# A top-p search on ScalarE: shorter arithmetic after each try, and two values made on VectorE

## The chip, the cores and the metric

The kernel runs on one core of a Trainium2 chip. The metric is the device time of one execution in microseconds (us), the median of several runs. Beside it stands one profiled execution, whose trace gives the start and length of every instruction.

Engines are named as the profile names them: PE (TensorE), PEld (its weight loads), DVE (VectorE), ACT (ScalarE), POOL (GpSimd), SP (SyncE). Each runs its own instructions in order and waits for others by semaphores.

## The reference

Two graph layers on N = 2708 nodes with D = 256 features, in float32. Cut to what matters:

```python
x = layernorm(x + relu(concat([x, adj @ x]) @ weight + bias))    # layer 0
R = adj + I;  R = R / R.sum(-1)
Xf = Xa = x
for n in range(2):                                               # layer 1
    q = Xa @ W1.T @ W2.T;  k = Xa @ W3.T
    probs = softmax(q @ k.T)                                     # N x N
    # nucleus (top-p): keep the largest probs of a row until their sum reaches 0.9
    A = probs * mask;  A = A / A.sum(-1)
    Xf = R @ Xf;  Xa = A @ Xa
    Z += Xf @ U1[n].T + Xa @ U2[n].T
h = layernorm(x + Z) * ln_g + ln_b
out = layernorm(x + h)
```

The part at issue is the mask of the second step (n = 1). It needs, for every row, the threshold at which the kept values reach 0.9 of the row's sum, without sorting 2708 values.

## The kernel before

Rows are worked on in 22 blocks of 128 rows (the last has 20). Block number t has a tile of 20 columns (`Block`, tile name `st` in the profile), one float per row and column: `z` (the row's sum of exponentials), `rz` (1/z), `nz` (-z), `l0`, `l1`, `l2` (three guesses, each z divided by the threshold guessed), `u0`, `u1` (l times the share of the row's sum that a try finds above its threshold), `n`, `kept`, `few`, `d`, `m` and others. All operations on them are one element wide. This tile has five buffers.

**The search of a block.** `begin_search` (VectorE, L893 to L898) makes `z`, `rz`, `nz` and the first guess `l0`. Two tries follow on ScalarE (`try_act`). A try k has two passes over the block's 2708 exponentials: L1027, Relu(e * l - z), and L1030, Sign of the same, each with a sum over the row (`relu`, `sign`). From these sums small operations make the next guess:

- L1033: n = 0.5 * sign + N/2
- L1035: u = relu * rz + n
- L1040: kept = l * (keep + 0.9 * slope) - down
- L1041: next l = -slope * u + kept
- L1043, in the second try alone: few = 0.9 * l1 - FEW

`keep`, `slope` and `down` are constants, one set for each try (`STEPS`). After that `last_level` (VectorE, L1064 to L1074) chooses the final level from `relu`, `rz`, `few` (L1064), `l1`, `u1` (L1066) and `l2`, and further values (L1068 on), and makes `d`. `below_level` (L1084) is a pass of VectorE over the block with `d`. Then VectorE takes candidates (L1091), sorts them (L1100, L1103), finds the threshold (L1119 to L1139), marks (L1144) and masks (L1149). L1149 writes the masked block that TensorE transposes (L562) and multiplies (L591).

**The loop and its order.** The order is written by hand. In period `per` the kernel has ScalarE try block per+1, VectorE finish the level of block per and the threshold of block per-1, TensorE multiply block per-2, and ScalarE form the exponentials of block per+2. A period has six slots g. In slot 0 ScalarE runs the first Relu pass, in slot 1 the first Sign pass and the small operations, in slots 2 and 3 the same of the second try. `begin_search` of block per+2 stands at the end of VectorE's slot 5, after `mask`; L882 (`shift`, the row maximum that the next exponentials L885 need) follows it in slot 0. Between its own work ScalarE copies TensorE's transposes out of PSUM (L564), one copy for each slot; TensorE can't go on without them.

**Beside it.** TensorE also works on the product R @ Xf in small units (L788). The rows for it are gathered by GpSimd (L745, DMA_INDIRECT, seven for a block of R). In the periods from 11 on GpSimd also does four operations of the last layer norm in a period (L1265, L1266), after which VectorE takes their statistics (L1240). SP issues the plain loads and stores.

**The first three blocks.** Block 0 makes its first try on VectorE (`try_dve`), its second try's sums partly on each, and `next_level` on ScalarE. `begin_search` of blocks 0, 1 and 2 runs ahead of the loop, around 706 to 716 us.

Of the kernel before, what the change touches and what calls it, by code (L numbers as in the profile page):

```python
# [11 lines left out]
AF = mybir.ActivationFunctionType  # L12
ALU = mybir.AluOpType
# [4 lines left out]
TOP_P = 0.9  # L18
# [15 lines left out]
STEPS = ((0.97048, 13.37709, 72.87486), (1.01755, 9.09506, 145.60103))  # L34
FEW = 17.8171
# [27 lines left out]
def gnn_two_layer_kernel(ctx: ExitStack, tc: tile.TileContext, N, xT_d, x_d, adj_d, w0_d, b0_d,  # L63
# [72 lines left out]
    with fast:  # L136
        fast_path(fast, tc, c, flags, fint, xT_d, x_d, w0_d, b0_d, w1_d, w2_d, w3_d, u1_d, u2_d, g_d, b_d)
# [22 lines left out]
def fast_path(ctx, tc, c, flags, fint, xT_d, x_d, w0_d, b0_d, w1_d, w2_d, w3_d, u1_d, u2_d, g_d, b_d):  # L160
    nc = tc.nc
    N, D, DA, NB, DC, KH, CHS, rows = c.N, c.D, c.DA, c.NB, c.DC, c.KH, c.CHS, c.rows
# [33 lines left out]
    b0 = es[1][:, :D]  # L196
# [328 lines left out]
    def logits(s, t, i):  # L525


        p = rows(t)
        lg = ps_lg()
        cs = KPS[2 * i:2 * i + 2]  # L530
        skip = CH - (cs[0][1] - cs[0][0])
        for h, (a, b) in enumerate(cs):
            o = slice(DA * h, DA * h + DA)
            at = (skip, 0)[h]
            nc.tensor.matmul(lg[:p, h, at:at + b - a], lhsT=q[o, t * P:t * P + p], rhs=keys[s][o, i, :b - a],  # L535
                             start=True, stop=True)
        a, b = cs[0][0], cs[-1][1]
        return lg.rearrange("p h n -> p (h n)")[:p, skip:skip + b - a], a, b
# [88 lines left out]
    def exps1(t):  # L627

        p = rows(t)
        e = es[t % 4]  # L630
        nmax, srt = st1[t]
        z = small.tile([P, 2], FP, tag="z1", name="z1", bufs=3)
        st1[t] = (srt, z)
        h = 11 * P

        def part(i):
            if i == 0:
                nc.scalar.activation(srt[:p], srt[:p], AF.Exp, bias=nmax[:p], scale=1.0)
            a, b = ((0, h), (h, N))[i]
            nc.scalar.activation(e[:p, a:b], e[:p, a:b], AF.Exp, bias=nmax[:p], scale=1.0,  # L640
                                 accum_out=z[:p, i:i + 1])
        return part
# [206 lines left out]
    def e2(t):  # L849
        return ring[t % 5]  # L850
# [40 lines left out]
    def begin_search(b):  # L891

        nc.vector.tensor_reduce(b.z, b.all[:b.p, :NL], AX.X, ALU.add)  # L893
        yield
        nc.vector.reciprocal(b.rz, b.z)
        nc.vector.tensor_scalar(b.nz, b.z, -1.0, None, op0=ALU.mult)
        yield
        nc.vector.tensor_scalar(b.l0, b.roots, b.roots, b.rz, op0=ALU.mult, op1=ALU.mult)  # L898

    def run_all(steps):  # L900
        for _ in steps:
            pass
# [22 lines left out]
    part = exps1(0)  # L925
# [5 lines left out]
    part = exps1(1)  # L931
# [11 lines left out]
    for t in range(NB):  # L943
        acc = ps_acc(t)
        part = exps1(t + 2) if t + 2 < NB else None
        b = None
        if t >= NB - 3:
            b = blocks[t - (NB - 3)] = Block(t - (NB - 3))
# [44 lines left out]
    scale, turn_out, project = ends  # L993
# [28 lines left out]
    def try_act(b, k, part):  # L1022


        e = e2(b.t)[:b.p, :N]
        if part == 0:
            nc.scalar.activation(scr[:b.p, :N], e, AF.Relu, bias=b.nz, scale=b.l[k], accum_out=b.relu)  # L1027
            return
        if part == 1:
            nc.scalar.activation(scr[:b.p, :N], e, AF.Sign, bias=b.nz, scale=b.l[k], accum_out=b.sign)  # L1030
            return
        if part == 2:
            nc.scalar.activation(b.n, b.sign, AF.Identity, bias=halfn[:b.p], scale=0.5)  # L1033
            return
        nc.scalar.activation(b.u[k], b.relu, AF.Identity, bias=b.n, scale=b.rz)  # L1035
        next_level(b, k)

    def next_level(b, k):
        keep, slope, down = STEPS[k]
        nc.scalar.activation(b.kept, b.l[k], AF.Copy, scale=keep + TOP_P * slope, bias=-down)  # L1040
        nc.scalar.activation((b.l1, b.l2)[k], b.u[k], AF.Identity, bias=b.kept, scale=-slope)  # L1041
        if k:
            nc.scalar.activation(b.few, b.l1, AF.Copy, scale=TOP_P, bias=-FEW)  # L1043

    def level(b, l):

# [275 lines left out]

    b0, b1, b2 = (blocks[t] for t in range(3))
    run_all(begin_search(b0))
    try_dve(b0, 0)
    run_all(begin_search(b1))
    try_dve(b0, 1)
    run_all(begin_search(b2))
    try_act(b0, 1, 0)
    next_level(b0, 1)  # L1330
    lg = logits(1, 3, 0)
    r_units(CC + 1)
    r_outs()
# [2 lines left out]
    for per in range(NB + 2):  # L1336
# [13 lines left out]
        for g in range(NG):  # L1350
# [26 lines left out]
            if b_act:  # L1377
                for k, part in {0: ((0, 0),), 1: ((0, 1), (0, 2), (0, 3)), 2: ((1, 0),), 3: ((1, 1), (1, 2), (1, 3))}.get(g, ()):
                    try_act(b_act, k, part)
# [19 lines left out]
    for f in later[0] + later[1]:  # L1399
# [10 lines left out]
                                   op0=ALU.mult, op1=ALU.is_lt)  # L1410
# [394 lines left out]
```

## Time and profile before

| | us |
|---|---|
| median of 6 runs (1255.69 to 1258.49) | 1256.62 |
| the profiled execution | 1256.08 |
| its span, first to last instruction | 1254.3 |
| TensorE busy in it | 1189.8 (95%) |
| VectorE busy | 975.4 (78%) |
| ScalarE busy | 734.7 (59%) |
| GpSimd busy | 637.5 (51%) |

| group | count | mean ns of one |
|---|---|---|
| L1027, L1030 ScalarE, 128x2708 | 41, 40 | 2641, 2642 |
| L1033 / L1035 / L1040 / L1041 / L1043 ScalarE, 128x1 | 40 / 40 / 41 / 41 / 21 | 294 / 386 / 186 / 295 / 187 |
| L895 / L896 / L898 VectorE, 128x1 | 21 / 21 / 21 | 164 / 134 / 273 |
| L1084, L1149 VectorE, 128x2720 | 21, 21 | 3041, 3055 |
| L745 GpSimd gather of `v_d` rows | 154 | 1281 |

How to read it: the shares are averages over the whole execution. The search runs only from about 700 us on; before that the first layer and the first step fill the time. Busy times of PE come from a model of pipelined matmuls. A line of the timeline has the start and the length in us, the engine, the line of the kernel, the operation, the tile written and the tiles read; a bracket at its end tells how long the engine had been idle and who ended that. An instruction's length reaches beyond the moment at which the engine takes up the next one, so that lengths of neighbours can overlap.

### The profile page before, as it was taken

To read this page: it belongs to the slowest core of one execution; us is meant where nothing else is said; L and a number is where in the kernel's file an instruction comes from. 1 tells how busy PE (TensorE), PEld (TensorE's weight loads), DVE (VectorE), ACT (ScalarE), POOL (GpSimd) and SP (SyncE) were. 2 spreads that over 40 slices of the span, in tenths; PEclk is the share of its full clock that TensorE was granted. 3 is DMA by queue.
4 is the path that set the end of the run, shared out by engine and by line. 5 is a ranking of instruction groups with operands and counts; after the bars stand their busy time and mean duration, and the time that the engine had idled before them with its cause. 6 is when DMAs were issued, how large, how long until landed. Compare 5 with 4: busy or idle time off the path is not lost.

```text
span 1254.3 us, 18668 instructions
## 1 busy us (share of the span) xinstructions
PE 1189.8 (95%) x5772; PEld 905.4 (72%) x5772; DVE 975.4 (78%) x3254; ACT 734.7 (59%) x1299; POOL 637.5 (51%) x596
## 2 busy tenths in 40 slices
PE   8999999999899999999999989999999999999885
PEld 6888878863477777777777667777766777766763
DVE  2455555784999998988861488989999999988796
ACT  2010110125466566666665498989989899988721
POOL 1000000004555552677676588788807888888850
PEclk9999999999899999999999999999999999999987
DMA  8475445433322220132334555655615555554441
GB/s 201 153 208 172 148 148 174 135 112 120 101 66 81 74 76 13 46 105 88 95 87 120 153 185 180 189 166 179 177 36 188 179 155 174 178 157 151 147 115 31
DMA packets 104248, 164.92 MB, mean 131 GB/s; under 512 B 20162, under 2 KB 76870, under 8 KB 104138
## 3 DMA queue, kind: packets, MB, share of 16 engines
q1 hardware_dynamic: 77852, 107.57, 26.9%
q0 software_dynamic: 20544, 51.17, 15.0%
q10 hardware_dynamic: 5742, 4.89, 1.4%
q8 instruction: 48, 0.79, 0.3%
q14 instruction: 62, 0.51, 0.1%
HBM read 129.66 MB, written 33.90 MB: 130 GB/s over the span
## 4 chain that ended last, share of the span: by engine, by line
PE 47%; ACT 8%; DVE 2%; POOL 2%; issue 1%; DMA 1%; POOLq 0%; ACTq 0%
PE acc L591 22%; PE misc L788 9%; PE lg L535 6%; PE tr L562 6%; ACT e L1030 2%; ACT e L885 1%; ACT e L1027 1%; PE misc L727 1%; POOL yg L745 1%; DVE e L1149 1%; PE acc L699 1%; ACT u L1250 1%; ACT wT L564 1%; ACT e L889 1%; DMA yg<-v_d,ix 1%
## 5 line engine op out<-in xcount | busy, mean ns | idle before, releaser
L564 ACT COPY wT<-tr 128x512 f32<-128x512 f32 (+2 forms) x258 | 136.6, 537 | 193.5 <-PE tr L562 193.4
L745 POOL DMA_INDIRECT yg<-v_d,ix x154 | 197.3, 1281 | 75.8 <-DMA v_d<-base 30.4
L591 PE MATMUL acc<-ya,wT 128*128 128x256 f32 x924 | 226.9, 388 | 0.0
L591 PE MATMUL acc<-x,wT 128*128 128x256 f32 x882 | 218.7, 388 | 0.0
L745 POOL DMA_INDIRECT yg<-yf_d,ix x154 | 188.9, 1227 | 55.8 <-issue 22.1
L274 PE MATMUL acc<-y,adj_t 128*128 128x257 f32 x924 | 204.4, 379 | 0.0
L591 PEld LDWEIGHTS acc<-x,wT 128*128 128x128 f32 x882 | 160.0, 191 | 59.2 <-issue 25.5
L591 PEld LDWEIGHTS acc<-ya,wT 128*128 128x128 f32 x924 | 174.1, 193 | 38.9 <-issue 16.7
L274 PEld LDWEIGHTS acc<-y,adj_t 128*128 128x128 f32 x924 | 173.6, 189 | 26.8 <-issue 1.9
L384 POOL DMA_INDIRECT adj_t<-in_adj,ix x154 | 164.5, 1068 | 51.6 <-issue 44.1
L562 PE MATMUL tr<-ident,e 128*128 128x128 f32 (+1 forms) x946 | 146.7, 274 | 17.2 <-DVE e L1149 12.1
L788 PE MATMUL misc<-yg,adj_t 128*128 128x256 f32 (+1 forms) x602 | 157.0, 389 | 0.9 <-DMA yg<-v_d,ix 0.8
L562 PEld LDWEIGHTS tr<-ident,e 128*128 128x128 f32 (+1 forms) x946 | 118.8, 143 | 51.3 <-issue 17.0
L535 PE MATMUL lg<-k,q 64*128 64x512 f32 (+3 forms) x528 | 136.5, 594 | 18.7 <-ACT e L889 7.6
L351 POOL DMA_DIRECT2D part_d<-e x1 | 0.6, 573 | 272.6 <-DVE e L350 272.6
L788 PEld LDWEIGHTS misc<-yg,adj_t 128*128 128x128 f32 (+1 forms) x602 | 104.7, 188 | 38.4 <-issue 16.8
L1027 ACT ACTIVATE e<-e,st 128x2708 f32<-128x2708 f32 (+1 forms) x43 | 113.6, 2641 | 0.0
L1030 ACT ACTIVATE e<-e,st 128x2708 f32<-128x2708 f32 (+1 forms) x42 | 111.0, 2642 | 0.0
L462 ACT COPY x1T<-tr 128x256 f32<-128x256 f32 (+1 forms) x22 | 8.0, 365 | 174.6 <-PE tr L461 174.6
L597 DVE MAX8 cand<-e 128x8 f32<-128x170 f32 (+1 forms) x352 | 86.3, 318 | 14.6 <-ACT e L542 14.5
L1091 DVE MAX8 cand<-w 128x8 f32<-128x170 f32 (+1 forms) x352 | 94.1, 321 | 0.1
L535 PEld LDWEIGHTS lg<-k,q 64*128 64x128 f32 (+1 forms) x528 | 38.9, 181 | 50.5 <-issue 20.9
(254 smaller groups left out, 1794.5 us busy)
## 6 DMA issues: line engine op xcount, KB each, us to landing
adj_t<-in_adj SPq DMA_DIRECT2D x42, 704.0 KB
adj_t<-adjc_d SPq DMA_DIRECT2D x44, 448.0 KB
adjc_d<-adj_t SPq DMA_DIRECT2D x22, 256.0 KB
base<-za_d SPq DMA_DIRECT2D x40, 128.0 KB
adjc_d<-adj_t SPq DMA_DIRECT2D x22, 192.0 KB
xt<-in_x ACTq DMA_DIRECT2D x21, 128.0 KB
x_d<-x SPq DMA_DIRECT2D x21, 128.0 KB
x1b_d<-xb SPq DMA_DIRECT2D x21, 128.0 KB
```

Source lines behind the costliest of these rows:

```text
L274: nc.tensor.matmul(acc[:p, :n], lhsT=halves[k // KH][:, k % KH, :p], rhs=y[:, k, :n], start=k == 0, stop=stop and k == NB - 1)
L384: nc.gpsimd.indirect_dma_start(out=a[:CW, i, :], out_offset=None, in_=adj_rows, in_offset=bass.IndirectOffsetOnAxis(ap=ix[:CW, m, i:i + 1] ...
L535: nc.tensor.matmul(lg[:p, h, at:at + b - a], lhsT=q[o, t * P:t * P + p], rhs=keys[s][o, i, :b - a], start=True, stop=True)
L562: nc.tensor.transpose(tr[:, k % 4, :p], columns(e[:p], k), ident[:p, :p])
L564: nc.scalar.copy(wT[:, :len(ks), :p], tr[:, :len(ks), :p])
L591: nc.tensor.matmul(acc[:p, :D], lhsT=wT[:, k % 4, :p], rhs=part_y(y, k), start=k == 0, stop=k == NB - 1)
L597: nc.vector.max(dst[:p, i * 8:(i + 1) * 8], src[:p, i * step:i * step + w])
L745: nc.gpsimd.indirect_dma_start(out=yg[:CW, m % 3, i, :], out_offset=None, in_=rows_d, in_offset=bass.IndirectOffsetOnAxis(ap=ix[:CW, m, i: ...
L788: nc.tensor.matmul(acc[:p, :D], lhsT=a[:kw, k, :p], rhs=y[:kw, k, :] if k < CC else own[:p], start=k == 0, stop=k == CC)
L1027: nc.scalar.activation(scr[:b.p, :N], e, AF.Relu, bias=b.nz, scale=b.l[k], accum_out=b.relu)
L1030: nc.scalar.activation(scr[:b.p, :N], e, AF.Sign, bias=b.nz, scale=b.l[k], accum_out=b.sign)
L1091: nc.vector.max(b.cand[:p, 8 * i:8 * i + 8], low[:p, SEG2 * i:SEG2 * (i + 1)])
```

## The change

In the first try ScalarE no longer forms u0. VectorE makes two values ahead, in `begin_search`: m = -slope * rz, and d = l0 * (keep + 0.9 * slope) - down - slope * N/2, in columns that the block has already. ScalarE then makes n = -slope/2 * sign + d and l1 = m * relu + n, which is the former l1 with its terms in another order. The operations `kept` (of the second try's constants) and `few` need only l1 and now come right after it, at the end of the first try (`from_level`). The second try then ends in n, u1 and l2. For one block ScalarE has seven small operations instead of nine, and VectorE two more. For blocks 0, 1 and 2 the two operations of VectorE are added ahead of the loop as well; block 0 doesn't use them.

```diff
@@ begin_search
         yield
+        keep, slope, down = STEPS[0]
         nc.vector.tensor_scalar(b.l0, b.roots, b.roots, b.rz, op0=ALU.mult, op1=ALU.mult)
+        nc.vector.tensor_scalar(b.m, b.rz, -slope, None, op0=ALU.mult)
+        nc.vector.tensor_scalar(b.d, b.l0, keep + TOP_P * slope, -down - slope * N / 2, op0=ALU.mult, op1=ALU.add)
@@ try_act
+        if part == 2 and k == 0:
+            nc.scalar.activation(b.n, b.sign, AF.Identity, bias=b.d, scale=-STEPS[0][1] / 2)
+            return
         if part == 2:
             nc.scalar.activation(b.n, b.sign, AF.Identity, bias=halfn[:b.p], scale=0.5)
             return
-        nc.scalar.activation(b.u[k], b.relu, AF.Identity, bias=b.n, scale=b.rz)
-        next_level(b, k)
-
-    def next_level(b, k):
-        keep, slope, down = STEPS[k]
-        nc.scalar.activation(b.kept, b.l[k], AF.Copy, scale=keep + TOP_P * slope, bias=-down)
-        nc.scalar.activation((b.l1, b.l2)[k], b.u[k], AF.Identity, bias=b.kept, scale=-slope)
-        if k:
-            nc.scalar.activation(b.few, b.l1, AF.Copy, scale=TOP_P, bias=-FEW)
+        if k == 0:
+            nc.scalar.activation(b.l1, b.relu, AF.Identity, bias=b.n, scale=b.m)
+            from_level(b)
+            return
+        nc.scalar.activation(b.u1, b.relu, AF.Identity, bias=b.n, scale=b.rz)
+        nc.scalar.activation(b.l2, b.u1, AF.Identity, bias=b.kept, scale=-STEPS[1][1])
+
+    def from_level(b):
+        keep, slope, down = STEPS[1]
+        nc.scalar.activation(b.kept, b.l1, AF.Copy, scale=keep + TOP_P * slope, bias=-down)
+        nc.scalar.activation(b.few, b.l1, AF.Copy, scale=TOP_P, bias=-FEW)
@@ before the loop
     try_act(b0, 1, 0)
-    next_level(b0, 1)
+    from_level(b0)
+    nc.scalar.activation(b0.l2, b0.u1, AF.Identity, bias=b0.kept, scale=-STEPS[1][1])
```

## The prediction

> **What bounds the kernel now.** I read the table of stages first, then the waits of each engine, then the chain of waits in order of time, then the timeline of single instructions. The change lives in the loop over 22 row blocks that begins near 721 us. In the table of stages the columns are: stretch, its length, then busy time (and instructions) of PE, PEld, DVE, ACT, POOL, then granted clock, DMA share and GB/s.
>
> ```profile
> 721.70:764.20 42.50, 34.43 (x149) 24.94 (x148) 33.89 (x115) 38.09 (x57) 34.28 (x28) 0.96 0.59 181
> 764.20:943.50 179.30, 178.26 (x878) 137.19 (x877) 165.00 (x564) 161.50 (x262) 120.09 (x98) 1.00 0.52 155
> 943.50:964.10 20.60, 18.08 (x89) 12.86 (x88) 18.52 (x64) 19.90 (x34) 16.64 (x14) 1.00 0.53 171
> 964.10:1018.00 53.90, 53.90 (x271) 42.40 (x269) 51.38 (x179) 49.42 (x82) 43.22 (x39) 1.00 0.58 179
> 1018.00:1089.40 71.40, 69.52 (x339) 52.95 (x339) 69.66 (x235) 68.52 (x115) 59.75 (x51) 1.00 0.55 161
> 1089.40:1191.70 102.30, 92.32 (x440) 72.41 (x438) 88.80 (x311) 87.77 (x154) 85.19 (x72) 0.97 0.52 160
> ```
>
> The reader is to see five regimes. 721.7 to 764.2 and 943.5 to 964.1: ScalarE is busiest (38.1 of 42.5, 19.9 of 20.6) and TensorE has gaps; the chain of waits passes through ScalarE's small operations at 727, 735, 749, 946 and 954 us. 764.2 to 943.5 and 964.1 to 1018: TensorE has hardly a gap (178.3 of 179.3, 53.9 of 53.9). 1018 to 1089.4: VectorE is busy 69.7 of 71.4, more than any other. From 1089.4 no engine is full, so a loop through several must bind. The waits of VectorE in the second and the sixth row tell the difference (total, times, longest):
>
> ```profile
> DVE st L1064 <- ACT st L1043: 8.7, 8, 1.5
> DVE bst L1240 <- POOL u L1266: 12.0, 8, 2.2
> ```
>
> Early, VectorE sits 1.1 us in most blocks waiting for ScalarE's last small operation (L1043): there it has slack. Late, it waits only for GpSimd. The starts of the masking pass L1149, once per block, are 994.01, 1017.97, 1042.24, 1066.20, 1089.37, 1115.01, 1140.67, 1166.33, 1191.72: intervals of about 24 us and then four of 25.4 to 25.7.
>
> What closes the late loop is seen in one block of the timeline (start, length, engine, line, operation):
>
> ```profile
> 1143.85 0.14 DVE L893 TENSOR_REDUCE bulk<-st 128x1 f32<-128x3 f32 x1
> 1144.02 0.16 DVE L895 RECIPROCAL st<-bulk 128x1 f32<-128x1 f32 x1
> 1144.10 0.13 DVE L896 TENSOR_SCALAR st<-bulk 128x1 f32<-128x1 f32 x1
> 1144.22 0.27 DVE L898 TENSOR_SCALAR st<-st 128x1 f32<-128x1 f32 x1
> 1144.41 0.27 DVE L882 TENSOR_REDUCE nmax<-lg 20x1 f32<-20x128 f32 x1
> ...
> 1147.04 3.05 DVE L1084 SCALAR_TENSOR_TENSOR w<-e,st 128x2720 f32<-128x2720 f32 x1
> ...
> 1162.50 0.43 DVE L1240 BATCH_NORM_STATS2 bst<-u 128x6 f32<-128x256 f32 x1 [2.15 <-POOL u L1266]
> ```
>
> ```profile
> 1146.10 0.95 POOL L745 DMA_INDIRECT yg<-v_d,ix  x1 [0.30 <-issue]
> 1147.35 3.55 POOL L745 DMA_INDIRECT yg<-v_d,ix  x1 [0.30 <-DMA yg<-v_d,ix]
> 1151.21 0.95 POOL L745 DMA_INDIRECT yg<-v_d,ix  x1 [0.31 <-PE misc L788]
> ```
>
> A gather that GpSimd begins 0.31 us after VectorE's long pass L1084 lasts 3.55 us instead of 0.95: it ends 0.8 after that pass. Then GpSimd works without a pause (seven gathers, four operations) until VectorE may go on at 1162.50 and 1164.00, then marks and masks (1166.33). So from the end of one mask to the end of the next all time is: VectorE's small operations up to L1084, L1084, GpSimd's queue, statistics, marks, mask. The chain of waits shows no semaphore between L1084 and the gather, yet VectorE's L893 to L898 stand in this loop.
>
> **ScalarE's part, step by step.** The second try now:
>
> ```profile
> 1164.41 0.18 ACT L1030 ACTIVATION_READ_ACCUMULATOR e<-e,st 128x1 f32 x1
> 1164.63 0.29 ACT L1033 ACTIVATE st<-st,halfn 128x1 f32<-128x1 f32 x1
> 1164.95 0.39 ACT L1035 ACTIVATE st<-st 128x1 f32<-128x1 f32 x1
> 1165.25 0.19 ACT L1040 ACTIVATE st<-st 128x1 f32<-128x1 f32 x1
> 1165.47 0.29 ACT L1041 ACTIVATE st<-st 128x1 f32<-128x1 f32 x1
> 1165.67 0.19 ACT L1043 ACTIVATE st<-st 128x1 f32<-128x1 f32 x1
> 1165.76 0.84 ACT L564 COPY wT<-tr 128x512 f32<-128x512 f32 x2
> ```
>
> An operation that needs the one before starts 0.03 after its end (L1033 to L1035: 0.33); one that doesn't starts 0.09 before its end (L1043 to the copy: 0.09). From the accumulator read to the copy: 1.35 us. New: read to n 0.21, n to u1 0.33, u1 to l2 0.39 + 0.03 = 0.42 (l2 now follows what it needs), l2 to the copy 0.20: 1.16, so 0.19 less. First try: now read 1156.24 to copy 1157.50, 1.26. New: 0.22, n to l1 0.33, l1 to kept 0.42, kept to few 0.09, few to copy 0.09: 1.15, so 0.11 less, since kept and few are not removed but moved here. Where no copy stands between (749 us) the next Relu needs l1 and starts 1.39 after the read; new 1.16, so 0.23 less.
>
> On the path: 727 (0.11), 735 (0.19), 749 (0.23), 946 (0.11), 954 (0.19): **0.83 us saved**. In the TensorE-bound stages nothing: ScalarE waits there 2.2 us per block for the transposes (914.20, L564), which hides any of it. From 1029 the chain of waits passes through five more first tries (1035, 1059, 1082, 1105, 1156; 0.11 each, 0.55 if all counted); I count nothing, because VectorE's queue ends later there.
>
> **VectorE's part.** m and d come after L898, one element wide. m starts 0.19 after L898, as L1058 does after L1055, a form like L898's (710.93 to 711.12). d reads l0 and so starts 0.31 after L898, as L1047 does (707.09 to 707.40). L882 starts 0.06 after d, as L1084 after L1280, of equal length 0.14 (1146.98 to 1147.04). L882 thus stands 0.37 after L898 instead of 0.19: **0.18 us per block**. Lower bound 0.11 (d not held by l0), upper 0.32 (0.31, then 0.20 as from L1047 to L1048); I take 0.18, since each step has a row of the same form.
>
> [...]
>
> Where it is on the path: after the masks from 1017.97 to 1166.33, seven blocks, 7 x 0.18 = **1.25 us lost** (0.8 to 2.2 by the bounds). Before 1018 it is hidden by VectorE's waits for L1043 (8.7 us in eight blocks) and for TensorE (L833, about 0.5 a block). Without that cover the 12 earlier blocks would cost 2.2 us more. The three searches begun at 706 to 716 us delay u1 for ScalarE's L1041 by some 0.5; ScalarE then waits 2.7 us for TensorE (719.37) anyway. L882's result is needed by the exponential at 1145.03; it lands at 1144.41 + 0.27 + 0.03 = 1144.71, and 0.18 later is still 0.14 early.
>
> **Waits that move.** L1064 needed L1043, the last of ScalarE's string; few and relu now come long before it. Its stall goes; next late are L1066 (u1) and L1068 (l2). Behind these wait the sorting operations and L1084. Around 910 us u1 would be there at 910.80 and l2 at 911.12, L1068 starting near 911.14 instead of 912.05. VectorE then waits 0.9 longer for TensorE at L833, so nothing comes of it. ScalarE's new needs, d and m, are written before nmax, which ScalarE has waited for earlier: no new stall.
>
> **Sum.** -0.83 + 1.25 = +0.4 us. Against the profiled execution (1256.08 us, span 1254.3, 1.8 around it) 1256.5. The median of the six runs, 1256.62, is 0.5 above that execution; on it: **1257.1 us**. A change of 0.2% (2.5 us) is about what these measurements can tell from none.
>
> **Rivals.** (1) *A gather slips in ahead.* In six of the seven blocks the gather starts 0.29 to 0.31 after L1084 (in the last 0.56). Long passes show both sides: at 739.66 a gather 0.21 after L1149 is held (3.67 us), at 795.04 one 0.08 after passes in 0.95, and the pass takes 3.10 instead of 3.05. Short passes narrow the border: L659 (519.51) is stretched from 0.285 to 0.353 by a gather 0.095 after it, L1070 is not by one 0.112 after it. With L1084 0.18 later the gathers stand at 0.11 to 0.13: held, by 0.02. If the two operations cost 0.20 or more, one gather more (0.95 + 0.30) is done under the long pass. Then three of the four late intervals shrink by 1.25 - 0.20 = 1.05, 3.15 in all, and the fourth grows by 0.20; the three before gain the 0.6 that VectorE waits for GpSimd there and lose 3 x 0.20. With the 0.83: -3.8, 1252.8 us. For it: so small a margin. Against it: the steps come from like rows, to about 0.02. [...]
>
> (2) *VectorE binds in every block* (slower). For it: it is busy 165.0 of 179.3 and 51.4 of 53.9 before 1018 too. Then all 19 blocks begun in the loop pay, 19 x 0.18 = 3.4, and ScalarE's savings fall away: 1260.0 us. It decides from the point where the stall before L1064 (1.15) and that before L833 (0.5) in a block are both used up. Against it: 0.18 doesn't reach 1.65, and the stall for L1043 shrinks with the change.
>
> (3) *ScalarE binds throughout*: 20 blocks x (0.11 + 0.19) = 6.0 saved, 1250.6 us. For it: 87.8 of 102.3 busy late, near VectorE's. Against it: its waits of 0.7 to 3.2 us for TensorE in almost every block.
>
> **How the numbers follow.** Forecast (the sum; its own range 1255.8 to 1258.6 from the bounds 0.8 to 2.2 and 0.55 more on ScalarE) 64%, rival 1 23%, rival 2 9%, rival 3 4%. The range reaches below rival 1, by 1.2 us should the blocked gather that follows cost less than counted, and leaves out rivals 2 and 3: 1251.6 to 1259.2. Faster by over 0.2%: 23 + 4 and 1 from the forecast's edge, 28%. Slower: 9 and 3 from the edge, 12%. The rest, 60%, within.
>
> **What would show it.** L898 to L882 at 0.37. Read to copy 1.15 and 1.16. L1064 without a stall before 1018, L833 with a longer one. Intervals of L1149 longer by 0.18 from 1018 on, and the gather at L1084 still 3.4 to 3.5 us long. A gather of 0.95 there followed by a held one, with intervals near 24.6, would be rival 1 and would make the prediction wrong, as would intervals longer by 0.18 before 1018.

## The result, and the profile after

The changed kernel takes 1260.36 us (median of 20 runs, 1256.92 to 1262.88), the kernel before 1256.92 in the same sets (41 runs, 1254.22 to 1258.97). The ratio is 1.0024, 95% interval 1.0017 to 1.0030: **3.0 us slower** by the ratio, 3.4 by the medians, where 0.4 was forecast and 1259.2 was the upper end of the range. The profiled execution took 1258.17 us, span 1256.3. In code lines from L898 on, the numbers are 1 to 8 higher now: l0 is L899, m L900, d L901, L1064 is L1072, L1084 is L1092, L1149 is L1157, L1240 is L1248, L1266 is L1274.

The waits of VectorE over the whole execution (total, times, longest), first before the change and then after it:

```profile
DVE bst L1240 <- POOL u L1266: 13.6, 11, 2.2
DVE st L1064 <- ACT st L1043: 13.0, 12, 1.8
DVE h L833 <- PE acc L591: 5.0, 9, 1.1
```

```profile
DVE bst L1248 <- POOL u L1274: 19.7, 15, 2.2
DVE h L833 <- PE acc L591: 10.0, 10, 1.1
DVE st L1072 <- ACT st L1045: 5.5, 9, 1.1
```

The wait for ScalarE shrank from 13.0 to 5.5 us. The wait for GpSimd's u (the tile that its four operations write) grew from 13.6 to 19.7 us and from 11 times to 15. In the table of stages (columns as before):

```profile
1017.20:1040.60 23.40, 22.87 (x112) 17.47 (x113) 22.37 (x82) 22.12 (x37) 19.72 (x17) 1.00 0.50 153
1040.60:1092.20 51.60, 49.81 (x240) 37.52 (x237) 44.86 (x160) 47.90 (x80) 43.03 (x37) 1.00 0.53 162
```

From 1018 to 1089 VectorE was busy 69.7 of 71.4. Now it is busy only 44.9 of 51.6 from 1040.6 on: the regime in which no engine is full begins at 1040.6 instead of 1089.4.

The starts of the masking pass give the place. Intervals in us, from mask to mask; then the distance from mask 3 to mask 19, which leaves out the prologue and the tail:

| kernel | 11-12 | 12-13 | 13-14 | 14-15 | 15-16 | 17-18 | mask 3 to 19 |
|---|---|---|---|---|---|---|---|
| before | 23.96 | 24.27 | 23.96 | 23.17 | 25.63 | 25.66 | 374.96 |
| after | 24.20 | 23.34 | **25.82** | **25.83** | 25.83 | 25.81 | 379.18 |
| end of the last u (L1266 / L1274) after the mask's start, before | 17.55 | 18.35 | 19.54 | 20.81 | 23.27 | 23.30 | |
| the same, after | 19.77 | 20.98 | 23.46 | 23.46 | 23.46 | 23.45 | |

GpSimd finishes its four operations 0.8 to 1.3 us later from block to block, in both kernels. When they end near 21 us after the mask, the next block's are what VectorE waits for, and the interval becomes 25.6 to 25.8. This is called the closed loop below: VectorE waits for GpSimd (2.15 us in a late block, before and after), and GpSimd's gather for VectorE's pass (3.55 us instead of 0.95 before the change, 3.72 after it). After the change GpSimd is 2.2 us later already in the interval from mask 11 to 12, so this happens two blocks sooner: 13-14 and 14-15 cost 1.86 + 2.66, 12-13 gives 0.93 back, the rest 0.6; 4.2 us in all. What comes back in 12-13 is VectorE's: GpSimd's four operations now begin 17.93 us after the mask, when four small operations of VectorE (L1137, L1142, L1144, L1147) are over, and these take 0.92 us together. Before (as L1129, L1134, L1136, L1139), they fell into the same 3.7 us as GpSimd's and took 2.73.

In a late block VectorE's part is as it was forecast. Here are its small operations, its long pass and the statistics, then GpSimd's gathers around the pass:

```profile
1147.42 0.27 DVE L899 TENSOR_SCALAR st<-st 128x1 f32<-128x1 f32 x1
1147.61 0.14 DVE L900 TENSOR_SCALAR st<-st 128x1 f32<-128x1 f32 x1
1147.73 0.15 DVE L901 TENSOR_SCALAR st<-st 128x1 f32<-128x1 f32 x1
1147.80 0.27 DVE L882 TENSOR_REDUCE nmax<-lg 20x1 f32<-20x128 f32 x1
...
1150.40 3.05 DVE L1092 SCALAR_TENSOR_TENSOR w<-e,st 128x2720 f32<-128x2720 f32 x1
...
1165.86 0.43 DVE L1248 BATCH_NORM_STATS2 bst<-u 128x6 f32<-128x256 f32 x1 [2.15 <-POOL u L1274]
```

```profile
1149.30 0.95 POOL L745 DMA_INDIRECT yg<-v_d,ix  x1 [0.30 <-issue]
1150.55 3.72 POOL L745 DMA_INDIRECT yg<-v_d,ix  x1 [0.30 <-PE misc L788]
```

L882 stands 0.38 after L899 (0.19 before), the gather 0.15 behind the pass is held for 3.72, and VectorE waits 2.15 for u, as it did. The late blocks, 0.16 longer, don't hold the loss.

Where GpSimd loses time is seen in the slots after masks 10 and 11. The timeline after mask 11 of the kernel before (start, length), VectorE first, then GpSimd:

```profile
998.51 0.22 DVE L1064 SCALAR_TENSOR_TENSOR st<-st 128x1 f32<-128x1 f32 x1 [0.29 <-ACT st L1043]
1000.79 3.04 DVE L1084 SCALAR_TENSOR_TENSOR w<-e,st 128x2720 f32<-128x2720 f32 x1
...
999.43 0.95 POOL L745 DMA_INDIRECT yg<-v_d,ix  x1 [0.30 <-issue]
1000.68 0.95 POOL L745 DMA_INDIRECT yg<-v_d,ix  x1 [0.30 <-PE misc L788]
1001.93 2.72 POOL L745 DMA_INDIRECT yg<-v_d,ix  x1 [0.30 <-issue]
```

And of the changed kernel:

```profile
997.36 0.20 DVE L1072 SCALAR_TENSOR_TENSOR st<-st 128x1 f32<-128x1 f32 x1
999.57 3.04 DVE L1092 SCALAR_TENSOR_TENSOR w<-e,st 128x2720 f32<-128x2720 f32 x1
...
998.46 0.95 POOL L745 DMA_INDIRECT yg<-v_d,ix  x1 [0.30 <-issue]
999.71 3.73 POOL L745 DMA_INDIRECT yg<-v_d,ix  x1 [0.30 <-PE misc L788]
1003.74 0.94 POOL L745 DMA_INDIRECT yg<-v_d,ix  x1 [0.30 <-PE misc L788]
```

Before, VectorE waited 0.29 for ScalarE, its long pass started at 1000.79, and a gather that started 0.12 ahead of it took 0.95; the next was held. Now that wait is gone, the pass starts 0.14 ahead of the gather, and that one is held to 0.8 after the pass's end. One gather less is done by then. After mask 10 it is the same (-0.17 before, +0.10 after). Counted from the start of the execution, GpSimd has 178 and 192 gathers (L745) behind it at the ends of these two passes, where it had 179 and 194 before: it loses one in each.

### The profile page after: what moved, and what is told of

The parts are those of the page before. It is cut to its first block, busy times and chain, and to the rows that moved or that the text cites. A ratio compares the mean times of both kernels' runs of the same rounds, so it can differ in the third digit from the quotient of the medians.

```text
span 1256.3 us, 18672 instructions
## 1 busy us (share of the span) xinstructions
PE 1188.3 (95%) x5772; PEld 904.2 (72%) x5772; DVE 976.1 (78%) x3298; ACT 728.7 (58%) x1257; POOL 647.5 (52%) x596
## 4 chain that ended last, share of the span: by engine, by line
PE 45%; ACT 8%; DVE 3%; POOL 2%; DMA 1%; issue 1%; POOLq 0%; ACTq 0%
PE acc L591 21%; PE misc L788 9%; PE lg L535 6%; PE tr L562 6%; ACT e L1033 2%; ACT e L1030 2%; DVE e L1157 1%; ACT e L885 1%; DMA yg<-v_d,ix 1%; PE misc L727 1%; PE acc L699 1%; ACT wT L564 1%; DVE w L1152 1%; ACT e L889 1%; POOL u L1274 1%
## 5 line engine op out<-in xcount | busy, mean ns | idle before, releaser
L745 POOL DMA_INDIRECT yg<-v_d,ix x154 | 202.2, 1313 | 69.4 <-PE lg L535 25.3
L745 POOL DMA_INDIRECT yg<-yf_d,ix x154 | 194.3, 1261 | 54.1 <-issue 26.3
```

Source lines behind the costliest of these rows:

```text
L745: nc.gpsimd.indirect_dma_start(out=yg[:CW, m % 3, i, :], out_offset=None, in_=rows_d, in_offset=bass.IndirectOffsetOnAxis(ap=ix[:CW, m, i: ...
```

## The experiments

Two theories stood against each other. **Theory P** (phase): the time goes because ScalarE's earlier end takes VectorE's wait away in the slots after masks 10 and 11, so that the long pass overtakes gathers. **Theory V**: the two small operations of VectorE are the loss.

| run | median | before, same set | ratio (95%) | mask 3 to 19 | closed from mask |
|---|---|---|---|---|---|
| e1_two_on_vector | 1257.48 | 1257.29 | 1.0001 (0.9991, 1.0010) | 376.11 | 15 |
| e2_few_first | 1258.36 | 1257.29 | 1.0013 (1.0004, 1.0022) | 376.83 | 14 |
| e3_few_last | 1261.34 | 1257.29 | 1.0033 (1.0021, 1.0045) | 379.16 | 13 |
| e4_two_idle | 1254.42 | 1257.29 | 0.9982 (0.9972, 0.9991) | 373.56 | never |
| e5_sort_ahead | 1251.17 | 1257.66 | 0.9944 (0.9930, 0.9957) | 369.69 | 16 |
| e6_sort_ahead_before | 1253.52 | 1257.66 | 0.9967 (0.9955, 0.9979) | 372.29 | 15 |
| e7_two_idle_in_two | 1256.82 | 1257.66 | 0.9992 (0.9980, 1.0004) | 375.77 | 15 |
| b_again (one execution) | 1256.93 | 1257.66 | | 374.97 | 15 |
| e11_scalar_late | 1255.36 | 1256.12 | 0.9993 (0.9985, 1.0002) | 376.02 | 15 |
| a_third | 1261.87 | 1256.12 | 1.0045 (1.0032, 1.0058) | 379.14 | 13 |

The last column is the first mask after which VectorE waits for u at both pairs of statistics, the closed loop over GpSimd.

### VectorE's part alone

```diff
 before, begin_search:
         nc.vector.tensor_scalar(b.l0, ...)
+        nc.vector.tensor_scalar(b.m, b.rz, -slope, None, op0=ALU.mult)
+        nc.vector.tensor_scalar(b.d, b.l0, keep + TOP_P * slope, -down - slope * N / 2, op0=ALU.mult, op1=ALU.add)
```

> The kernel before with VectorE's two operations m and d alone (written, not read; ScalarE as before). Theory P (phase: the change costs time because the stall that VectorE had before L1064 goes, so that its long pass L1084 overtakes gathers in blocks 10 to 12 and the loop closed by GpSimd begins two blocks sooner): here ScalarE's last small operation still ends last, the stall of 0.46 and 0.29 us in blocks 10 and 11 shrinks by 0.19 at most and the gathers still start ahead of L1084; the interval after masks 13 and 14 stays near 24 us. Only the 0.18 to 0.19 per block from mask 12 on is paid: 7 x 0.18 = +1.3 us against the kernel before, about 1258, and the intervals late are 25.8. Theory V (the two operations are the whole loss of the change, ScalarE's edit is worth nothing or a gain): as slow as the changed kernel or slower, +3 us or more, with the interval of 25.8 from mask 13 on.

The time is that of the kernel before, and the closed loop begins at mask 15 as there. Mask 3 to 19 takes 1.15 us more, close to the forecast's 1.25 for this part. The interval of the ratio, 1.1 us below to 1.3 above, holds both that and nothing. Theory V falls.

### few alone moved

```diff
 before, next_level:
-        if k:
+        if k == 0:
             nc.scalar.activation(b.few, b.l1, AF.Copy, scale=TOP_P, bias=-FEW)
```

(Block 0, whose first try is VectorE's, gets its few after its `next_level`.)

> The kernel before with one line moved: ScalarE makes few at the end of the first try instead of at the end of the second; no added work on any engine. Theory P: VectorE's stall before L1064 goes, L1084 comes earlier in blocks 10 to 12 (3.3 to 3.4 us after the mask's end instead of 3.7 to 3.8), a gather that started 0.12 to 0.17 ahead of it is now 0.2 to 0.3 behind it and is held, and the loop closed by GpSimd begins at mask 13 or 14 instead of 15: slower by 1 to 4 us, intervals late unchanged at 25.66. Theory V: VectorE has no work more, ScalarE's string in the second try is shorter by 0.1: not slower, 0 to -0.6 us.

Slower, with no operation more on any engine: 1.6 us by the ratio. After mask 10 a wait of 0.56 stays and the gather passes; after mask 11 no wait is left. There the timeline has:

```profile
1001.15 3.04 DVE L1084 SCALAR_TENSOR_TENSOR w<-e,st 128x2720 f32<-128x2720 f32 x1
...
1000.16 0.95 POOL L745 DMA_INDIRECT yg<-v_d,ix  x1 [0.30 <-issue]
1001.41 3.60 POOL L745 DMA_INDIRECT yg<-v_d,ix  x1 [0.30 <-PE misc L788]
```

One gather lost (0.26 after the pass's start instead of 0.12 ahead), one block sooner in the closed loop. This is theory P in the small, in one of the two slots that had been expected.

### few back at the end, in the changed kernel

```diff
 after, from_level:
-        nc.scalar.activation(b.few, b.l1, AF.Copy, scale=TOP_P, bias=-FEW)
 after, try_act, end of the second try:
         nc.scalar.activation(b.l2, b.u1, AF.Identity, bias=b.kept, scale=-STEPS[1][1])
+        nc.scalar.activation(b.few, b.l1, AF.Copy, scale=TOP_P, bias=-FEW)
```

> The changed kernel with few moved back to the end of the second try (m, d and the short strings stay). Theory P: VectorE stalls again before its first operation of the last level where ScalarE is late (blocks 1 to 11), its long pass comes 3.6 us or more after the mask's end in blocks 10 and 11, the gathers get ahead of it, and the loop closed by GpSimd begins later: 1 to 3.5 us faster than the changed kernel, 1257 to 1259 at the most. Theory V: the two operations are still there: no gain against the changed kernel (within 0.5 us), so 0.2 to 0.3% slower than the kernel before.

A miss: no gain. The trace says why the edit didn't do what it was for: after mask 10 few ends at 973.77 and VectorE's first operation that reads it starts at 973.80, its own time. No wait came back, the pass starts 3.52 and 3.49 us after the masks, and both gathers are held. The expectation had put the wait down to the place of one operation; with that one back in its place, the rest of ScalarE's shortening (both tries) was enough to end the wait in both slots. The run left open whether ScalarE's end is the cause; e11 answers that.

### Two idle operations ahead of the long pass

```diff
 after, vector_slots:
         if a:
+            nc.vector.tensor_scalar(a.g, a.d, 1.0, None, op0=ALU.mult)
+            nc.vector.tensor_scalar(a.g, a.g, 1.0, None, op0=ALU.mult)
             below_level(a)
```

> The changed kernel with two more small VectorE operations (one element wide, their result unread, the second needs the first) right ahead of the long pass L1092 in every block. In the changed kernel the gathers start 0.125 to 0.14 us after that pass begins and are held 3.73 us. Theory P: the pass comes 0.3 us later, the gather starts ahead of it and takes 0.95, the next one is held to the same end (pass end + 0.82), so GpSimd does one gather more per block, worth 1.25 us: intervals of the late loop 25.82 + 0.3 - 1.25 = 24.9, and the late loop begins later: faster than the changed kernel by 5 us or more, 1252 to 1255, faster than the kernel before too. Theory V (each small operation of VectorE costs its time from mask 12 on): slower than the changed kernel by 8 x 0.3 = 2.4 us or more, 1262 to 1263.

More work on VectorE, and 2.3 us faster than the kernel before. A late block of its timeline:

```profile
1148.96 0.15 DVE L1206 TENSOR_SCALAR st<-st 128x1 f32<-128x1 f32 x1
1149.14 0.15 DVE L1207 TENSOR_SCALAR st<-st 128x1 f32<-128x1 f32 x1
1149.21 3.04 DVE L1092 SCALAR_TENSOR_TENSOR w<-e,st 128x2720 f32<-128x2720 f32 x1
...
1149.11 0.95 POOL L745 DMA_INDIRECT yg<-v_d,ix  x1 [0.30 <-PE misc L788]
1150.36 2.71 POOL L745 DMA_INDIRECT yg<-v_d,ix  x1 [0.30 <-issue]
```

The pass starts 0.25 later after the mask (3.74 instead of 3.49); that is enough for a gather to go first. VectorE never waits for u, and sets the interval itself: 24.66. Some 1.8 us of that go with GpSimd all the same. Lines of such a block show it; behind them stand the same three of VectorE's lines in the changed kernel after mask 12:

```profile
1109.86 0.52 DVE L1142 TENSOR_TENSOR_SCAN sc<-bulk,sc 128x3 f32<-128x3 f32 x1
1110.41 0.68 DVE L1144 TENSOR_TENSOR part<-sc,ranks 128x32 f32<-128x32 f32 x1
1111.12 0.77 DVE L1147 TENSOR_SCALAR part<-part,st 128x32 f32<-128x32 f32 x1
...
1109.63 0.72 POOL L1276 TENSOR_TENSOR u<-u,x1b 128x256 f32<-128x256 f32 x1
1110.31 0.73 POOL L1275 TENSOR_TENSOR u<-u,gb 128x256 f32<-128x256 f32 x1
1111.12 0.73 POOL L1276 TENSOR_TENSOR u<-u,x1b 128x256 f32<-128x256 f32 x1
```

```profile
1033.25 0.23 DVE L1142 TENSOR_TENSOR_SCAN sc<-bulk,sc 128x3 f32<-128x3 f32 x1
1033.51 0.19 DVE L1144 TENSOR_TENSOR part<-sc,ranks 128x32 f32<-128x32 f32 x1
1033.73 0.24 DVE L1147 TENSOR_SCALAR part<-part,st 128x32 f32<-128x32 f32 x1
```

With L1137 (0.76 to 0.78 instead of 0.27) these small operations of VectorE take 1.8 us longer in a block where GpSimd's four fall beside them. In the closed loop GpSimd's come later, while VectorE waits (2.15 us for u in the changed kernel's late block).

### A sorting operation moved ahead of the pass

```diff
 after, vector_slots (and, in e6_sort_ahead_before, the kernel before):
-        run_all(turns((part_of_it(order, 7) if b else None, 1), (levels, 1)))
+        run_all(turns((part_of_it(order, 8) if b else None, 1), (levels, 1)))
```

> The changed kernel with one sorting operation (a match-and-replace of the block ahead, 0.3 us) taken from behind the long pass L1092 to ahead of it: no work added, nothing left out. Theory P: the pass comes 0.32 us later (3.8 after the mask's end instead of 3.49), a gather that started 0.13 behind it now starts 0.19 ahead, and GpSimd's loop no longer closes: no wait of VectorE for GpSimd's u at bn_stats, intervals about 24.4 us (the 24.66 of the kernel with two idle operations less the 0.25 that these took), 1.7 us less than that kernel: about 1252.5, 6 us or more faster than the changed kernel and 4 faster than the kernel before. If instead the late loop closes over GpSimd also with the gather ahead, the interval stays 24.6 to 24.7 and the time 1254 to 1255.

> The kernel before with the same sorting operation moved ahead of its long pass L1084. Theory P: the gather that stood 0.30 behind that pass now starts at about -0.02, so it goes first where it stays below 0.08; VectorE then sets the interval, which has no m and d in it: 24.4 - 0.18 = 24.2, and the time is 1251 to 1253, as fast as the changed kernel with the same move or up to 1 us faster. If ScalarE's shorter strings are worth something once GpSimd is out of the way, it is 1 to 2 us slower than that kernel. If -0.02 isn't enough, the gathers are held and the time stays at 1257.

Both are faster, by 7.0 and 4.1 us by their ratios; the first is the fastest kernel of this study and computes the same. VectorE's wait for GpSimd in it is 8.2 us instead of 19.7:

```profile
DVE bst L1248 <- POOL u L1274: 8.2, 9, 1.2
```

It had been expected to vanish, and doesn't: from mask 16 the loop closes over GpSimd again, but with a gather more ahead of the pass, at 24.96. In e6 it closes too, where an interval of 24.2 set by VectorE had been expected. The numbers follow from the changed kernel's: the closed interval is 25.82 + (start of the long pass after the mask's end - 3.49) - 1.25 for each gather that gets ahead. It gives 25.65 for the kernel before (3.32; measured 25.66), 24.96 for this one (3.88), 24.83 for e6 (3.75; 24.83 to 24.87). That e6 is slower than e5 isn't settled as a worth of ScalarE's edit: after masks 10 and 11 the held gather starts 0.76 and 0.79 into the pass in e6 and 1.04 and 1.00 into it in e5, so GpSimd's place differs there too.

### The two slots alone, from VectorE's side

```diff
 after, vector_slots:
         if a:
+            if b and b.t in (11, 12):
+                nc.vector.tensor_scalar(a.g, a.d, 1.0, None, op0=ALU.mult)
+                nc.vector.tensor_scalar(a.g, a.g, 1.0, None, op0=ALU.mult)
             below_level(a)
```

> The changed kernel with the two idle small operations ahead of the long pass in two blocks only, the ones after masks 10 and 11, where the kernel before still had its stall of 0.46 and 0.29 us and let a gather pass. Theory P: a gather passes in each of the two again (0.95 us, at -0.04 to -0.12), GpSimd is two gathers further, the loop closed by GpSimd begins at mask 14 or 15 instead of 13, late intervals 25.82 as in the changed kernel: 1.5 to 4 us faster than the changed kernel, 1256.5 to 1259. Theory V, or the phase of these two blocks not being what decides: 0.5 us slower than the changed kernel or equal to it, 1260 to 1261, with 25.8 from mask 13 on.

Four tiny operations in the whole execution, and the loss is gone. The gathers stand at -0.08 and -0.13, the closed loop begins at mask 15, and its intervals are 25.80, those of the changed kernel.

### Second traces of both kernels

> The kernel before once more, unchanged, for a second trace: its masks should come at the same distances from mask 1 on to some 0.1 us, the gathers ahead of L1084 in blocks 10 and 11, the interval of 25.6 from mask 15 on. The first part up to mask 0 and the tail after mask 21 (24.8 us in the first trace, 23.6 in the changed kernel) may differ by 1 to 2 us from one execution to the next; if so, these parts of the two kernels' difference are not the change's.

The kernel before gave 374.97 us from mask 3 to 19, after 374.96 in its first trace, and the changed kernel 379.14 (a_third) after 379.18: the pattern is reproduced to 0.05 us. From mask 19 to the end the kernels take 60.6 to 64.8 us in no order that follows the edits, so totals of single executions aren't compared here.

### One idle operation, two sorting operations

e8 is the kernel with one idle operation instead of two; e10 takes `part_of_it(order, 9)`. With them the changed kernel ran once more (a_again) and e9, below. This set ran on a chip on which the kernel before took 1312.31 us, with VectorE's waits of up to 6.7 us and intervals of up to 38.8 us between masks 0 and 11 that no other trace has; mask 0 itself comes at 775 to 780 us there instead of 738 to 741.

> The changed kernel with one idle small VectorE operation ahead of the long pass in every block (the kernel before last in this series had two, worth 0.25 us together). Theory P with the border between a gather that passes and one that is held at 0.08 to 0.10 us after the pass begins: the gather moves from 0.135 to about 0.0, so it passes; VectorE has 0.12 us a block less to do than with two: about 1253.5, a us faster than with two. If the border lies below 0.0, the gathers are held and the time is 1260 to 1262.

> The changed kernel with two sorting operations moved ahead of the long pass instead of one. So far the late interval followed 25.82 + (start of the pass after the mask's end - 3.49) - 1.25 for a gather more that gets ahead. With two the pass starts 4.2 after the mask's end, the number of gathers ahead of it is the same as with one (the next stands at +0.7 and is held 3.2): 25.82 + 0.7 - 1.25 = 25.27, against 24.97 with one: 1 to 2 us slower than with one, 1252 to 1253.5. If the hold were a fixed time instead of lasting to the pass's end, the interval would stay at 24.97 and the time at 1251.

Both ratios are near those of the other kernels with a later pass (0.9972, 0.9946 to 0.9998; 0.9979, 0.9951 to 1.0007) and, with these pauses, tell little. That of e8 lies below 1 although its gathers were held, where a time above the kernel before had been expected; this stays open. The traces tell more. In e10 the closed interval is 25.30, where 25.27 was worked out: the hold does last to the pass's end (in the two traces of the result every gather held at L1084 or L1092 ends 0.81 to 0.83 after it), and a pass put later than the gather needs costs its whole delay. In e8 one operation moved the pass by 0.06, not 0.12, so the gathers start 0.073 to 0.083 after it and are held (3.79 to 3.78 us long); one at 0.064 passed (0.95). The expectation had put the border at 0.08 to 0.10. The closed interval of e8 is 25.88.

> The changed kernel once more, for a second trace: from mask 3 to mask 19 it should again take 379.2 us against 375.0 in both traces of the kernel before, with 25.8 from mask 13 on; the part up to mask 3 and the tail after mask 19 (61.1 us) may differ by 1 to 2 us from one execution to the next.

After the pause at mask 9 (interval 32.4) GpSimd had caught up and the changed kernel's closed loop began at mask 15 there. That the loss hangs on where GpSimd stands, and not on the edit's own operations, fits this too; the comparison of lengths that this run was for can't be made.

### ScalarE late in the two slots

```diff
 after, from_level:
+        if b.t not in (12, 13):
             nc.scalar.activation(b.few, b.l1, AF.Copy, scale=TOP_P, bias=-FEW)
 after, try_act, end of the second try:
+        if b.t in (12, 13):
+            nc.scalar.activation(b.half, b.l2, AF.Copy, scale=1.0, bias=0.0)
+            nc.scalar.activation(b.half, b.half, AF.Copy, scale=1.0, bias=0.0)
+            nc.scalar.activation(b.few, b.l1, AF.Copy, scale=TOP_P, bias=-FEW)
```

> The changed kernel in which, for two blocks only, ScalarE makes few last again and does two idle small operations before it, so that VectorE's first operation of the last level waits for ScalarE in the slots after masks 10 and 11, as it did in the kernel before; VectorE's work is that of the changed kernel. In the run that moved few alone it came 0.03 us before VectorE wanted it, so no wait came back; with 0.5 to 0.7 us more on ScalarE it does. Theory P: a stall of 0.4 to 0.6 us there, a gather passes in each of the two slots, the loop over GpSimd begins at mask 14 or 15: 1.5 to 4 us faster than the changed kernel although ScalarE does more. If ScalarE's end doesn't decide this, the time is that of the changed kernel, 1260 to 1261, or 0.5 more.

In the set just told the ratio was 1.0023 (1.0001 to 1.0045), with the pause right before the two slots; no verdict. The same kernel again, beside the changed one:

> The kernel in which ScalarE ends later in the two slots after masks 10 and 11 once more (its first run met an execution at 1316 us beside 1312 for the kernel before, with waits of 4 to 6 us for nmax around mask 9 that no earlier trace has, so that the two slots it is about came after a pause that had let GpSimd catch up). Beside a kernel before at about 1257: theory P: L1072 waits 0.4 to 0.6 us in both slots, a gather passes in each, the interval of 25.8 begins at mask 14 or 15 instead of 13, and the time is 1.5 to 4 us below that of the changed kernel in the same set. If ScalarE's end isn't what decides: the time of the changed kernel or 0.5 above.

> The changed kernel in the same set as the one before, for comparison: 1.0017 to 1.0030 of the kernel before; from mask 3 to mask 19 about 379.2 us, with the interval of 25.8 from mask 13 on.

e11 is 6.5 us below the changed kernel in the same set by the medians, more than the 4 expected, and a_third is further above the kernel before than the 20 runs of the result (1.0045 instead of 1.0024). By the distance from mask 3 to 19 they differ by 3.1. The two profiled executions took about the same (1258.09 and 1257.93), since that of e11 came to mask 3 1.7 us later and had a tail 1.5 longer, for which no cause was looked for. After mask 11, e11's timeline:

```profile
999.72 0.22 DVE L1077 SCALAR_TENSOR_TENSOR st<-st 128x1 f32<-128x1 f32 x1 [0.25 <-ACT st L1050]
1001.95 3.05 DVE L1097 SCALAR_TENSOR_TENSOR w<-e,st 128x2720 f32<-128x2720 f32 x1
...
1000.50 0.95 POOL L745 DMA_INDIRECT yg<-v_d,ix  x1 [0.30 <-issue]
1001.75 0.95 POOL L745 DMA_INDIRECT yg<-v_d,ix  x1 [0.30 <-PE misc L788]
1003.00 2.81 POOL L745 DMA_INDIRECT yg<-v_d,ix  x1 [0.30 <-issue]
```

VectorE waits 0.25 for few (L1050), the pass starts 0.20 after the gather, and this is the picture of the kernel before. After mask 10 it waits 0.76. The last u ends 17.64 us after mask 11 instead of 19.77. ScalarE alone was made slower, in two of 22 blocks, and the changed kernel is no slower than the kernel before (0.9985 to 1.0002): theory P is shown from both engines.

## Why the prediction was wrong, step by step

- **ScalarE's strings**: 1.15 and 1.16 us were worked out from the read to the next operation; 1159.45 to 1160.62, 1167.53 to 1168.70 and 747.86 to 749.03 are 1.17 each. Right.
- **0.83 us saved ahead of 964**: mask 3 comes at 816.07 and 816.31 in two traces of the changed kernel, at 816.76 and 816.87 in two of the kernel before. But e7 and e11, the same code up to there, have 817.88 and 818.04. Not settled for the 0.53 of it that was forecast at 727 to 749. The 0.30 at 946 and 954 is seen: mask 9 to 11 takes 44.10 and 44.03 us instead of 44.38 and 44.40.
- **VectorE's 0.18 a block**: from l0 to nmax 0.377 to 0.380 instead of 0.190, late intervals 25.82 instead of 25.66. As a term, 1.25 was forecast; e1 has 1.15 between masks 3 and 19, and e11 1.06 with the 0.30 just told in it. Right. But the sign "the gather at L1084 still 3.4 to 3.5 us long" didn't follow from the prediction's own reading: a gather that ends 0.8 after the pass is held longer when the pass starts later, 3.72 to 3.74 in the late blocks.
- **The wait at L1064**: it was to go. In the blocks from mask 3 to 7 0.42 of 1.15 stayed, now for u1 (L1045): the prediction looked at what L1064 reads, but the code has it write n, which ScalarE's u1 still reads. After masks 10 and 11 the wait did go. The wait at L833 rose from 0.5 to 1.1, and the intervals stayed 22.28. In the stage bound by TensorE nothing came of it, as forecast.
- **The failed step** is the sentence "VectorE then waits 0.9 longer for TensorE at L833, so nothing comes of it", and with it a sum that has no term for the block at which the closed loop begins. It looked at what waits for VectorE and not at what VectorE's pass keeps waiting. After masks 10 and 11 the pass now starts 3.53 and 3.48 us after the mask's end instead of 3.79 and 3.74, ahead of the gather instead of behind it. The rows were there in the trace of before: gathers 0.17 and 0.12 ahead of L1084, after waits of 0.46 and 0.29 that the change was said to end. The term left out is the 3.1 us between e11 and the changed kernel. With it the way from mask 3 to 19 adds up: 1.06 + 3.12 = 4.2 us, as measured. That the whole is 3.0 to 3.4 would need some 1 us less outside of it; 0.53 was forecast there, and the traces don't settle it.
- **The range**: the forecast's own range was added up wrongly. From 1256.62 the bounds give 1256.0 to 1258.0, not 1255.8 to 1258.6; the stated range reached further anyway.
- **Rival 1** had the right mechanism in the wrong place and direction: it asked whether the late pass, moved later, would let a gather in, and not whether the earlier pass, moved earlier, would shut one out. Its margin of 0.02 was in truth some 0.05: at L1084 and L1092 gathers up to 0.071 after the pass's start went through, at 0.073 two did (e4, e6) and one was held (e8), and later ones were all held; the late ones of the changed kernel stood at 0.125 to 0.143. With 0.25 us more (e4) it came true, at 1254.42 against the 1252.8 worked out for it. In the traces of the two kernels the hold goes one way: a gather that starts 0.10 to 1.29 us into L1084 or L1092 ends 0.81 to 0.83 after that pass, but a long pass that starts while a gather runs takes 3.03 to 3.05 us, as one without a gather does (3.03 at 913.49 in the kernel before), and two into whose start a gather slips there took 3.07 (780.85) and 3.10 (794.97). VectorE's small operations beside GpSimd's four arithmetic ones, in contrast, do take longer (L1144 0.68 us in e4 instead of 0.19).
- **Rivals 2 and 3** did not occur: from mask 3 to 8 the intervals stayed at 22.28, and VectorE still waits in each of them.

## What to carry to other kernels

When an edit takes a wait away, look at what the freed engine starts next and at every queue that its next long instruction can hold (here a gather took 3.73 us instead of 0.95): a wait that costs nothing may be what keeps the order of two engines, as VectorE's 0.46 and 0.29 us for ScalarE did here. In a loop with a growing backlog a loss of 1.25 us in one block can bring the closed regime a whole block sooner (e2), so count at which block the regime begins as well as what its period is. And once the order has been found, set it by moving work that is there anyway: one sorting operation put ahead of the pass made 7 us.

## What was not expected of the hardware

A difference of some hundredths of a microsecond decides 1.25 us: at L1084 and L1092 a gather 0.071 us after the pass's start took 0.948, one 0.073 after it 0.947 in e6 and another 0.073 after it 3.788 in e8. At the masking pass the border lies higher, since gathers at 0.079 to 0.088 still took 0.94 to 0.95 and one at 0.107 was held for 3.765; why it differs was not looked into.
